# An adapter kept in two tables: biases carried as rows and added by TensorE, two gathers in place of five, the last sequence's base products as tasks of their own

## Chip, cores and metric

The kernel runs on one core of a Trainium2 chip. The metric is the device time of one execution in microseconds (us), the median of several runs. The core has a matrix engine (TensorE, PE in the profile; PEld is its weight load), a vector engine (VectorE, DVE), a scalar engine (ScalarE, ACT), a general engine (GpSimd, POOL) and a queue engine for transfers (SyncE, SP). Matrix products land in PSUM, of which this kernel uses eight banks of 128 x 512 floats.

## What is computed

The reference is one decoder layer on eight sequences of 512 tokens and 256 channels, all in float32: a linear attention with an MLP, a cross-attention over a context of 512 tokens, and a feed-forward part with adapters. Each of the three is followed by x = layernorm(x + part(x)). The change touches the third part only:

```python
base = jnp.einsum('btd,de->bte', x, W_base) + b_base
h = relu(jnp.einsum('btd,ndh->nbth', x, W_enc) + b_enc[:, None, None, :])
recon = jnp.einsum('nbth,nhd->nbtd', h, W_dec) + b_dec[:, None, None, :]
losses = jnp.mean((recon - x[None]) ** 2, axis=(2, 3))
top1 = jnp.argmin(losses, axis=0)
adp = connected_idx[top1]
mid = relu(jnp.einsum('btd,bdr->btr', x, W_down[adp]) + b_down[adp][:, None, :])
adapter_out = jnp.einsum('btr,brd->btd', mid, W_up[adp]) + b_up[adp][:, None, :]
return base + adapter_out
```

For every sequence eight small autoencoders (256 to 64 to 256 channels) try to rebuild the tokens. The one with the smallest error names an adapter, whose two matrices (256 x 64 and 64 x 256) and two biases are then applied to the whole sequence. Which one it is, is known only at run time, so the weights are fetched by an index.

## The kernel before

A sequence x is held as four tiles of 128 tokens x 256 channels (NT = 4). Channels are cut in two chunks of 128 (KC = 2). A float32 product shows as two matrix passes in the profile, so a product over both chunks is four.

**The order of the work** is written by a planner inside the kernel, at build time. Every piece of work is a task (`task`, L112) with an engine, a cost in ns, a due time, what it reads and writes, and the buffers ("rooms") that it fills. `play` (L157) walks through a planned time: whenever an engine is free, it picks, among the tasks that are ready and whose rooms are free, the one with the smallest due time (plus a small bonus or penalty for the change of kind, `SWAY`). It does not look ahead. What it picks is issued at once on that engine, so each engine's order of instructions is the order of the plan, and on the chip each engine follows that order and waits where its data or buffer is late:

```python
fit = [k for k in ready[e]
       if k.at + k.on[e][1] <= now and (port <= now or not alone(k, e)) and roomy(k, now)]
...
k = min(fit, key=lambda k: k.due + SWAY[e].get((was[e], k.kind), 0.0))
```

A task with `others` can go to a second engine after a delay; the bias adds, for instance, are POOL tasks which DVE may take. PSUM has four rooms called "bank" for most products and two double rooms "sc" for attention scores. The queue of SP is planned too: it carries the loads of x and of the context, the stores of the results (L1066, L1060) and the copies of `place` (L904 to L915), 16 transfers which move a transposed block of attention weights into place and which the planner books at 9600 ns.

**The sequences overlap.** Sequence b has its cross-attention in period b (64 x 3.2 us planned); its feed-forward part (`ffn`, L957) runs during the next period, beside the cross-attention of b + 1 and the linear attention of b + 2. Only the last sequence's `ffn` has nothing beside it.

**The steps of `ffn`.** (1) `turn` (L422) transposes x into x2T. (2) Four POOL adds put the base bias on x (L962 to L966; recorded at L377). (3) Four encode products (L973), each for two autoencoders, with a ReLU on ACT (L981) into one of two rooms "he". (4) Eight decode pairs (`decode`, L1070): a pair is two products (L1076) in two banks, which must both be free, each followed by a subtraction on DVE (L1086) into a room "h", of which there are four, and a sum of squares on ACT (L1093). (5) A product with ones (L994) spreads the eight losses over all partitions, and `choose` (L1099) finds the adapter's index with nine small DVE instructions and works out row numbers. (6) Five gathers on POOL (L1001) fetch the down matrix in two halves (128 rows of 64 floats each), the down bias, the up matrix (64 rows of 256 floats) and the up bias, 128 times the same row of 256 floats. (7) The middle product (L1019) with ReLU and bias on ACT (L1023). (8) For each of the four tiles: a POOL add of the up bias to x (L1028, recorded at L377), base and up products in one bank (L1038, L1039), a DVE add to x (L1045) and the statistics of the final norm (L388, L389). (9) The norm: ve on DVE (L397), the power -0.5 on POOL (L402, "rs"), the normalisation (`put`: L410 on DVE, L414 on POOL), and the store. For the last sequence norm and store go tile by tile, for the others all four tiles at once.

The norm that ends the cross-attention has the same form (L397, L402, L410, L414).

Of the kernel before, what the change touches and what calls it, by code (L numbers as in the profile page):

```python
# [9 lines left out]
F32 = mybir.dt.float32  # L10
# [8 lines left out]
P = 128  # L19
# [14 lines left out]
EPS = 1e-5  # L34

# [29 lines left out]
def decoder(ctx: ExitStack, tc: tile.TileContext, t: dict, out: bass.AP):  # L65
# [186 lines left out]
    room("bu", 1, [P, C])  # L252
# [68 lines left out]
    Wbase, bbase = chunked("Wbase", C, C), row("bbase", C)  # L321
# [17 lines left out]
    )  # L339

    row_base = const.tile([P, 4], F32, name="row_base")
    row_step = const.tile([P, 4], F32, name="row_step")
    for j, (start, per, step) in enumerate([(0, 1, C), (P, 1, C), (0, 1, R), (0, 0, 1)]):
        nc.gpsimd.iota(
            row_base[:, j : j + 1],
            [[0, 1]],
            base=start,
            channel_multiplier=per,
            allow_small_or_imprecise_dtypes=True,
        )  # L350
# [606 lines left out]
    def ffn(b, begin, end):  # L957
        x2, x2T, acc, part = xs[b], Val("xT"), Val("acc"), Val("part")
        long = end - begin
        turn(x2T, x2, begin)  # L960
        for c in range(NT):
            task(  # L962
                "pool", 728, begin + (0.1 + 0.05 * c) * long,
                lambda e, c=c: add(e, x2.t[:, c, :], x2.t[:, c, :], bbase),
                [(x2, c)], [(x2, c)], ("bbase",), others=[("dve", 420, 4000)], two=True,
            )  # L966
# [24 lines left out]
        ps_l, bu, mid = Val("bank"), Val("bu"), Val("h")  # L991
# [5 lines left out]
        task("dve", 1900, begin + 0.61 * long, lambda: rows.append(choose(b, ps_l.t)), [(ps_l, 0)], [(chosen, 0)])  # L997
# [9 lines left out]
        every = slice(None)  # L1007
        due = begin + 0.63 * long
        for kc in range(KC):
            task("pool", 1000, due, gather(lambda kc=kc: wd[:, kc, :R], Wdown_rows, every, slice(kc, kc + 1)),  # L1010
                 [(chosen, 0)], [(v_wd, kc)], slack=2000)
        task("pool", 1000, due + 1, gather(lambda: bd[:R], bdown_rows, slice(0, R), slice(2, 3)), [(chosen, 0)], [(v_bd, 0)], slack=2000)
        task("pool", 1000, due + 2, gather(lambda: wu[:R], Wup_rows, slice(0, R), slice(2, 3)), [(chosen, 0)], [(v_wu, 0)], slack=2000)
        task("pool", 1000, due + 3, gather(lambda: bu.t, t["bup"], every, slice(3, 4)), [(chosen, 0)], [(bu, 0)], slack=2000)
        ps_m = Val("bank")

        def middle():
            for kc in range(KC):
                nc.tensor.matmul(ps_m.t, wd[:, kc, :], x2T.t[:, kc, :], start=kc == 0, stop=kc == KC - 1)  # L1019

        task("pe", mm(512, 2), begin + 0.8 * long, middle, chunks(x2T) + each(v_wd, KC), [(ps_m, 0)], kind="full", holds=[mid])
        task(
            "act", 686, begin + 0.82 * long, lambda: nc.scalar.activation(mid.t, ps_m.t, AF.Relu, bias=bd),  # L1023
            [(ps_m, 0), (v_bd, 0)], [(mid, 0)],
        )
        norm = Norm(x2)
        for c in range(NT):
            task(  # L1028
                "pool", 723, begin + 0.8 * long + c,
                lambda e, c=c: add(e, x2.t[:, c, :], x2.t[:, c, :], bu.t),  # L1030
                [(x2, c), (bu, 0)], [(x2, c)], others=[("dve", 420, 4000)], two=True,
            )
            ps = Val("bank")

# [161 lines left out]
```

## Time and profile before

| | us |
|---|---|
| three runs | 1677.8, 1677.01, 1680.26 |
| median | 1677.8 |
| profiled execution, its own time | 1677.12 |
| its span, first to last instruction | 1675.3 |
| busy: PE / DVE / ACT / POOL | 1569.5 / 1320.5 / 1084.0 / 1075.2 |
| mean granted TensorE clock | 0.972 of full speed |

How to read it: an engine line of the page gives busy time and its share of the span. In the view of 40 slices each digit is a busy share in tenths. A group or timeline line has the start, the duration, the engine, the line of the kernel, the operation and the buffers as out<-in, followed by the shape and the number of instructions merged; the bracket holds the time that the engine stood idle before it and what ended that. "SPq" is SyncE's queue of transfers, whose time is that of issuing them. Buffers are named by their rooms, so prods stands for several buffers that share the space of the attention products.

### The profile page before, as it was taken

The page shows a single profiled execution, that of the slowest core. Times are in us where ns is not written, and L with a number is a line of the kernel's source. Part 1 is how long each engine was busy: PE and PEld are TensorE (multiplying, and loading weights), DVE is VectorE, ACT ScalarE, POOL GpSimd, SP SyncE. Part 2 cuts the span into 40 slices and gives each one's busy share as a digit, 9 for nine tenths or more (in the row PEclk, how much of TensorE's full clock was granted, in tenths as well). Part 3 has the DMA queues.
Part 4 walks back from the last instruction along what each step waited for, and adds up shares of the span by engine and source line. Part 5 has one row for each costly group of instructions (what it writes and reads, how often), then busy time and mean ns, then how long its engine had stood idle before and what let it go on. Part 6 is the DMA issues. An engine that isn't in the chain of part 4 may idle for free.

```text
span 1675.3 us, 23902 instructions
## 1 busy us (share of the span) xinstructions
PE 1569.5 (94%) x7856; PEld 935.4 (56%) x7856; DVE 1320.5 (79%) x2261; ACT 1084.0 (65%) x2359; POOL 1075.2 (64%) x881
## 2 busy tenths in 40 slices
PE   4489999999999999999998999989999899999996
PEld 2366666664665555565565565655566554654562
DVE  7987886798889898979976797868969566776554
ACT  1147776678676787678756677657766567646643
POOL 6955886686678697669565794758938241544243
PEclk8689999999999999999999999999999999999998
DMA  8000000022113211221113121221112322333301
GB/s 267 1 1 1 1 1 0 8 54 58 33 34 88 52 26 38 53 75 51 48 29 89 46 52 30 59 79 28 51 35 55 88 72 68 80 100 91 91 7 32
DMA packets 159003, 86.68 MB, mean 52 GB/s; under 512 B 18336, under 2 KB 156192, under 8 KB 158880
## 3 DMA queue, kind: packets, MB, share of 16 engines
q1 hardware_dynamic: 157472, 83.06, 18.4%
q0 software_dynamic: 1408, 2.10, 0.6%
q8 instruction: 63, 1.03, 0.3%
q14 instruction: 60, 0.49, 0.1%
HBM read 16.93 MB, written 4.19 MB: 13 GB/s over the span
## 4 chain that ended last, share of the span: by engine, by line
PE 74%; DVE 10%; SPq 4%; issue 3%; ACT 3%; POOL 3%; DMA 2%; POOLq 0%; DVEq 0%; ACTq 0%
PE sc L847 12%; PE bank L929 12%; PE bank L687 7%; PE bank L662 6%; PE bank L945 5%; PE bank L793 5%; PE bank L893 5%; PE bank L511 4%; SPq L913 4%; PE bank L973 3%; PE bank L800 3%; PE bank L1076 3%; PE bank L809 3%; DVE o L591 2%; ACT p L862 2%
## 5 line engine op out<-in xcount | busy, mean ns | idle before, releaser
L862 ACT ACTIVATE p<-sc,nmax 128x512 f32<-128x512 f32 x512 | 348.1, 689 | 111.3 <-DVE nmax L854 88.6
L873 POOL TENSOR_SCALAR p<-p,rinv 128x512 f32<-128x512 f32 x284 | 204.5, 731 | 325.6 <-DVE rinv L867 316.5
L854 DVE TENSOR_REDUCE nmax<-sc 128x2 f32<-128x1024 f32 x256 | 304.9, 1213 | 82.7 <-PE sc L847 82.0
L559 POOL TENSOR_TENSOR prods<-k,v 128x1088 f32<-128x1088 f32 x119 | 297.5, 2523 | 59.8 <-DVE k L537 32.6
L847 PE MATMUL sc<-kT,qT 64*128 64x512 f32 x1024 | 265.5, 627 | 5.5 <-ACT p L862 4.3
L582 POOL TENSOR_TENSOR prods<-q,kv 128x1088 f32<-128x1088 f32 x95 | 237.4, 2519 | 37.3 <-DVE kv L568 25.6
L568 DVE TENSOR_REDUCE kv<-prods 128x68 f32<-128x1088 f32 x128 | 162.3, 1273 | 10.9 <-POOL prods L559 10.5
L893 PEld LDWEIGHTS bank<-ident,p 128*128 128x128 f32 x1072 | 121.7, 141 | 80.4 <-issue 45.7
L591 DVE TENSOR_REDUCE o<-prods 128x68 f32<-128x1088 f32 x128 | 160.6, 1271 | 4.5 <-POOL prods L582 4.5
L871 ACT ACTIVATE p<-p,rinv 128x512 f32<-128x512 f32 x228 | 155.5, 730 | 3.2 <-DVE rinv L867 2.7
L893 PE MATMUL bank<-ident,p 128*128 128x128 f32 x1072 | 150.3, 277 | 2.6 <-ACT qT L804 1.1
L847 PEld LDWEIGHTS sc<-kT,qT 64*128 64x128 f32 x1024 | 88.7, 190 | 109.6 <-issue 77.2
L929 PE MATMUL bank<-prods,v 128*64 128x256 f32 x1008 | 127.9, 397 | 16.0 <-DMA prods<-blk 14.7
L883 DVE STREAM_TRANSPOSE blk<-p 128x512 f32<-128x512 f32 x184 | 121.9, 689 | 25.7 <-POOL p L873 11.0
L929 PE MATMUL bank<-pT,v 128*64 128x256 f32 x1040 | 128.0, 388 | 4.0 <-DMA prods<-prods 2.1
L793 PE MATMUL bank<-x1T,Wq 128*128 128x512 f32 (+1 forms) x288 | 124.1, 554 | 1.0 <-DVE x L1045 0.5
L945 PE MATMUL bank<-Wo,oT 128*128 128x256 f32 x512 | 121.1, 382 | 0.0
L687 PE MATMUL bank<-projT,h 128*128 128x256 f32 x512 | 119.1, 383 | 1.3 <-ACT h L723 1.3
L687 PEld LDWEIGHTS bank<-projT,h 128*128 128x128 f32 x512 | 95.3, 190 | 26.0 <-issue 9.2
L945 PEld LDWEIGHTS bank<-Wo,oT 128*128 128x128 f32 x512 | 94.8, 190 | 26.5 <-issue 12.1
L929 PEld LDWEIGHTS bank<-prods,v 128*64 128x64 f32 x1008 | 70.2, 141 | 70.6 <-issue 29.6
L372 ACT COPY oT<-bank 128x256 f32<-128x256 f32 x100 | 37.2, 372 | 110.2 <-PE bank L929 109.7
(142 smaller groups left out, 2859.1 us busy)
## 6 DMA issues: line engine op xcount, KB each, us to landing
prods<-blk SPq DMA_DIRECT2D x480, 64.0 KB, 2.1
pT<-blk SPq DMA_DIRECT2D x256, 64.0 KB, 2.1
prods<-prods SPq DMA_DIRECT2D x176, 64.0 KB, 2.1
pT<-prods SPq DMA_DIRECT2D x64, 64.0 KB, 2.1
x<-in_x SPq DMA_DIRECT2D x7, 512.0 KB, 6.5
out<-x SPq DMA_DIRECT2D x7, 512.0 KB, 3.4
ctx<-in_ctxT SPq DMA_DIRECT2D x8, 256.0 KB, 3.1
fcT<-in_fcT SPq DMA_DIRECT2D x1, 1024.0 KB
```

Of the source, the lines that this page charges most:

```text
L559: (nc.gpsimd if e == "pool" else nc.vector).tensor_tensor(pr.t.rearrange("p (d e h) -> p d e h", d=DSPLIT, h=H1), k.t[:, s : s + DSPLIT, : ...
L582: (nc.gpsimd if e == "pool" else nc.vector).tensor_tensor(pr.t.rearrange("p (h e d) -> p h e d", h=DSPLIT, d=D1), q.t[:, s : s + DSPLIT, : ...
L591: nc.vector.tensor_reduce(o.t[:, s : s + DSPLIT, :], pr.t.rearrange("p (h e d) -> p h e d", h=DSPLIT, d=D1), AX.X, ALU.add)
L687: nc.tensor.matmul(ps.t[:, :C], of(f, c), projT[:, f, :], start=f == fs[0], stop=f == fs[-1])
L793: nc.tensor.matmul(ps_q.t[:, :n], Wq[:, kc, cols], x1T.t[:, kc, rows], start=kc == 0, stop=kc == KC - 1)
L847: nc.tensor.matmul(ps.t[:, i, :], qT.t[rows, c * P : (c + 1) * P], kT.t[rows, :], start=True, stop=True)
L854: lambda: nc.vector.tensor_reduce(nmax.t, ps.t, AX.X, ALU.max, negate=True), [(ps, 0)], [(nmax, 0)],
L862: lambda i=i, p=p: nc.scalar.activation(p.t, ps.t[:, i, :], AF.Exp, bias=nmax.t[:, i : i + 1], accum_out=ssum.t[:, i : i + 1]),
L873: nc.gpsimd.tensor_scalar(p.t, p.t, rinv.t[:, i : i + 1], 1.0, ALU.mult, ALU.mult)
L893: nc.tensor.transpose(bank.t[:, m * P : (m + 1) * P], p.t[:, m * P : (m + 1) * P], ident)
L929: nc.tensor.matmul(to, v2.t[:, m, cols], of, start=m == 0, stop=m == NT - 1)
L945: nc.tensor.matmul(ps.t[:, :C], oT.t[:, c * P : (c + 1) * P], Wo[:, pr, :], start=pr == prs[0], stop=pr == prs[-1])
```

## The change

The host lays an adapter out in two tables. `down` has, per adapter, 128 rows of 257 floats: both chunks of the down matrix, padded with zeros from 64 to 128 columns, and as last column the down bias, then ones in rows 64 and 65, then zeros. `up` has 66 rows of 256 floats per adapter: the up matrix, the up bias, the base bias. The ReLU over the middle product, with the last column of `down` as its bias, leaves two rows of ones in mid at 64 and 65, and the up product adds both biases through them. The POOL adds of the base bias and of the up bias go, and so do the load of the base bias and the room "bu". Two gathers fetch what five did. `choose` reads the losses where they lie in PSUM, and its two index steps are folded into one by a second table of -8 to -1, so seven DVE instructions stand for nine; its planned cost goes from 1900 to 1500.

For the last sequence alone (`final`) the tiles go in pairs that share a bank, and the base products become a task without the adapter as input, due at 0.6 of the part's length; the up products are a second task into the same bank. For the other sequences base and up stay one task per tile.

```diff
+UP = 66
...
-    room("bu", 1, [P, C])
...
-    Wbase, bbase = chunked("Wbase", C, C), row("bbase", C)
+    Wbase = chunked("Wbase", C, C)
...
+    iota_low = const.tile([P, NA], F32, name="iota_low")
+    nc.gpsimd.iota(
+        iota_low, [[1, NA]], base=-NA, channel_multiplier=0, allow_small_or_imprecise_dtypes=True
+    )
+    row_base = const.tile([P, 2], F32, name="row_base")
+    row_step = const.tile([P, 2], F32, name="row_step")
+    nc.gpsimd.iota(row_base, [[0, 2]], base=0, channel_multiplier=1, allow_small_or_imprecise_dtypes=True)
+    for j, step in enumerate((P, UP)):
         nc.gpsimd.memset(row_step[:, j : j + 1], float(step))
-    Wdown_rows = t["Wdown"].rearrange("n d r -> (n d) r")
-    Wup_rows = t["Wup"].rearrange("n r d -> (n r) d")
-    bdown_rows = t["bdown"].rearrange("n (r o) -> (n r) o", o=1)
-    wd = const.tile([P, KC, P], F32, name="wd")
+    down_rows = t["down"].rearrange("n p m -> (n p) m")
+    up_rows = t["up"].rearrange("n r d -> (n r) d")
+    wd = const.tile([P, KC * P + 1], F32, name="wd")
     wu = const.tile([P, C], F32, name="wu")
-    bd = const.tile([P, 1], F32, name="bd")
-    for z in (wd, wu, bd):
-        nc.gpsimd.memset(z, 0.0)
+    nc.gpsimd.memset(wu, 0.0)
...
     def ffn(b, begin, end):
         x2, x2T, acc, part = xs[b], Val("xT"), Val("acc"), Val("part")
-        long = end - begin
+        long, final = end - begin, b == B - 1
         turn(x2T, x2, begin)
-        for c in range(NT):
-            task(
-                "pool", 728, begin + (0.1 + 0.05 * c) * long,
-                lambda e, c=c: add(e, x2.t[:, c, :], x2.t[:, c, :], bbase),
-                [(x2, c)], [(x2, c)], ("bbase",), others=[("dve", 420, 4000)], two=True,
-            )
         NG = NA * R // P
         for g in range(NG):
             ps, he = Val("bank"), Val("he")
...
             lambda: nc.vector.tensor_tensor(part.t, acc.t[:, :, 0], acc.t[:, :, 1], ALU.add),
             [(acc, (a, kc)) for a in range(NA) for kc in range(KC)], [(part, 0)],
         )
-        ps_l, bu, mid = Val("bank"), Val("bu"), Val("h")
+        ps_l, mid = Val("bank"), Val("h")
         task(
             "pe", 100, begin + 0.6 * long,
             lambda: nc.tensor.matmul(ps_l.t[:, :NA], ones, part.t, start=True, stop=True), [(part, 0)], [(ps_l, 0)], kind="full",
         )
         rows = []
-        task("dve", 1900, begin + 0.61 * long, lambda: rows.append(choose(b, ps_l.t)), [(ps_l, 0)], [(chosen, 0)])
+        task("dve", 1500, begin + 0.61 * long, lambda: rows.append(choose(b, ps_l.t)), [(ps_l, 0)], [(chosen, 0)])
         def gather(dst, src, lo, hi):
             def emit():
...
             return emit
-        every = slice(None)
         due = begin + 0.63 * long
-        for kc in range(KC):
-            task("pool", 1000, due, gather(lambda kc=kc: wd[:, kc, :R], Wdown_rows, every, slice(kc, kc + 1)),
-                 [(chosen, 0)], [(v_wd, kc)], slack=2000)
-        task("pool", 1000, due + 1, gather(lambda: bd[:R], bdown_rows, slice(0, R), slice(2, 3)), [(chosen, 0)], [(v_bd, 0)], slack=2000)
-        task("pool", 1000, due + 2, gather(lambda: wu[:R], Wup_rows, slice(0, R), slice(2, 3)), [(chosen, 0)], [(v_wu, 0)], slack=2000)
-        task("pool", 1000, due + 3, gather(lambda: bu.t, t["bup"], every, slice(3, 4)), [(chosen, 0)], [(bu, 0)], slack=2000)
+        task("pool", 1000, due, gather(lambda: wd, down_rows, slice(0, P), slice(0, 1)), [(chosen, 0)], [(v_wd, 0)], slack=2000)
+        task("pool", 1000, due + 1, gather(lambda: wu[:UP], up_rows, slice(0, UP), slice(1, 2)), [(chosen, 0)], [(v_wu, 0)], slack=2000)
         ps_m = Val("bank")
         def middle():
             for kc in range(KC):
-                nc.tensor.matmul(ps_m.t, wd[:, kc, :], x2T.t[:, kc, :], start=kc == 0, stop=kc == KC - 1)
-        task("pe", mm(512, 2), begin + 0.8 * long, middle, chunks(x2T) + each(v_wd, KC), [(ps_m, 0)], kind="full", holds=[mid])
-        task(
-            "act", 686, begin + 0.82 * long, lambda: nc.scalar.activation(mid.t, ps_m.t, AF.Relu, bias=bd),
-            [(ps_m, 0), (v_bd, 0)], [(mid, 0)],
+                nc.tensor.matmul(ps_m.t, wd[:, kc * P : (kc + 1) * P], x2T.t[:, kc, :], start=kc == 0, stop=kc == KC - 1)
+        task("pe", mm(512, 2), begin + 0.8 * long, middle, chunks(x2T) + [(v_wd, 0)], [(ps_m, 0)], kind="full", holds=[mid])
+        task(
+            "act", 686, begin + 0.82 * long, lambda: nc.scalar.activation(mid.t, ps_m.t, AF.Relu, bias=wd[:, KC * P :]),
+            [(ps_m, 0), (v_wd, 0)], [(mid, 0)],
         )
         norm = Norm(x2)
-        for c in range(NT):
-            task(
-                "pool", 723, begin + 0.8 * long + c,
-                lambda e, c=c: add(e, x2.t[:, c, :], x2.t[:, c, :], bu.t),
-                [(x2, c), (bu, 0)], [(x2, c)], others=[("dve", 420, 4000)], two=True,
-            )
+        for cs in ((0, 1), (2, 3)) if final else ((0,), (1,), (2,), (3,)):
             ps = Val("bank")
-            def base(c=c, ps=ps):
-                cols = slice(c * P, (c + 1) * P)
-                for kc in range(KC):
-                    nc.tensor.matmul(ps.t[:, :C], x2T.t[:, kc, cols], Wbase[:, kc, :], start=kc == 0, stop=False)
-                nc.tensor.matmul(ps.t[:, :C], mid.t[:, cols], wu, start=False, stop=True)
-            due = begin + (0.86 + 0.03 * c) * long
-            task("pe", mm(256, 3), due, base, chunks(x2T, [c]) + [(mid, 0), (v_wu, 0)], [(ps, 0)], ("Wbase",), "full")
-            task(
-                "dve", 416, due + 0.02 * long,
-                lambda c=c, ps=ps: nc.vector.tensor_tensor(x2.t[:, c, :], x2.t[:, c, :], ps.t[:, :C], ALU.add),
-                [(ps, 0), (x2, c)], [(x2, c)],
-            )
-            norm.stats(c, due + 0.03 * long)
-        final = b == B - 1
+            def base(cs=cs, ps=ps):
+                for n, c in enumerate(cs):
+                    for kc in range(KC):
+                        nc.tensor.matmul(
+                            ps.t[:, n * C : (n + 1) * C], x2T.t[:, kc, c * P : (c + 1) * P], Wbase[:, kc, :],
+                            start=kc == 0 and n == 0, stop=False,
+                        )
+            def up(cs=cs, ps=ps):
+                for n, c in enumerate(cs):
+                    nc.tensor.matmul(
+                        ps.t[:, n * C : (n + 1) * C], mid.t[:, c * P : (c + 1) * P], wu, start=False, stop=c == cs[-1]
+                    )
+            due = begin + (0.86 + 0.03 * cs[-1]) * long
+            if final:
+                task("pe", mm(256, 4), begin + (0.6 + 0.01 * cs[-1]) * long, base, chunks(x2T, cs), [(ps, 0)], ("Wbase",), "full")
+                task("pe", mm(256, 2), due, up, [(mid, 0), (v_wu, 0)], [(ps, 0)], kind="full")
+            else:
+                task("pe", mm(256, 3), due, lambda f=base, g=up: (f(), g()), chunks(x2T, cs) + [(mid, 0), (v_wu, 0)],
+                     [(ps, 0)], ("Wbase",), "full")
+            for n, c in enumerate(cs):
+                task(
+                    "dve", 416, due + 0.02 * long,
+                    lambda n=n, c=c, ps=ps: nc.vector.tensor_tensor(
+                        x2.t[:, c, :], x2.t[:, c, :], ps.t[:, n * C : (n + 1) * C], ALU.add
+                    ),
+                    [(ps, 0), (x2, c)], [(x2, c)],
+                )
+                norm.stats(c, due + 0.03 * long)
...
     def choose(b, ps):
-        loss = small.tile([P, NA], F32, tag="loss", name=f"loss_{b}")
-        nc.vector.tensor_copy(loss, ps[:, :NA])
         least = small.tile([P, 1], F32, tag="least", name=f"least_{b}")
-        nc.vector.tensor_reduce(least, loss, AX.X, ALU.min)
+        nc.vector.tensor_reduce(least, ps[:, :NA], AX.X, ALU.min)
         pick = small.tile([P, NA], F32, tag="pick", name=f"pick_{b}")
-        nc.vector.tensor_scalar(pick, loss, least, -float(NA), ALU.is_equal, ALU.mult)
+        nc.vector.tensor_scalar(pick, ps[:, :NA], least, -float(NA), ALU.is_equal, ALU.mult)
         nc.vector.tensor_tensor(pick, pick, iota_a, ALU.add)
         first = small.tile([P, 1], F32, tag="first", name=f"first_{b}")
         nc.vector.tensor_reduce(first, pick, AX.X, ALU.min)
-        nc.vector.tensor_scalar(first, first, float(NA), None, ALU.add)
-        nc.vector.scalar_tensor_tensor(pick, iota_a, first, cidx, ALU.is_equal, ALU.mult)
+        nc.vector.scalar_tensor_tensor(pick, iota_low, first, cidx, ALU.is_equal, ALU.mult)
         adp = small.tile([P, 1], F32, tag="adp", name=f"adp_{b}")
         nc.vector.tensor_reduce(adp, pick, AX.X, ALU.add)
-        rows = small.tile([P, 4], I32, tag="rows", name=f"rows_{b}")
+        rows = small.tile([P, 2], I32, tag="rows", name=f"rows_{b}")
         nc.vector.scalar_tensor_tensor(rows, row_step, adp, row_base, ALU.mult, ALU.add)
         return rows
...
+    down = np.zeros((NA, P, KC * P + 1), np.float32)
+    for kc in range(KC):
+        down[:, :, kc * P : kc * P + R] = a["ffn_W_down"][:, kc * P : (kc + 1) * P]
+    down[:, :R, -1] = a["ffn_b_down"]
+    down[:, R:UP, -1] = 1.0
+    b_base = np.broadcast_to(a["ffn_b_base"], (NA, 1, C))
+    up = np.concatenate([a["ffn_W_up"], a["ffn_b_up"][:, None], b_base], axis=1)
```

The planner's constants, the periods and everything outside this part are unchanged.

More of the change, by code (lines that the diff above doesn't have):

```diff
@@ L339, in decoder @@
     )
[L341 to L349, printed above, removed]
-        )
+    iota_low = const.tile([P, NA], F32, name="iota_low")
[6 more added lines that the diff above has]
+    for j, step in enumerate((P, UP)):
         nc.gpsimd.memset(row_step[:, j : j + 1], float(step))
-    Wdown_rows = t["Wdown"].rearrange("n d r -> (n d) r")
-    Wup_rows = t["Wup"].rearrange("n r d -> (n r) d")
-    bdown_rows = t["bdown"].rearrange("n (r o) -> (n r) o", o=1)
-    wd = const.tile([P, KC, P], F32, name="wd")
+    down_rows = t["down"].rearrange("n p m -> (n p) m")
+    up_rows = t["up"].rearrange("n r d -> (n r) d")
+    wd = const.tile([P, KC * P + 1], F32, name="wd")
     wu = const.tile([P, C], F32, name="wu")
-    bd = const.tile([P, 1], F32, name="bd")
-    for z in (wd, wu, bd):
-        nc.gpsimd.memset(z, 0.0)
+    nc.gpsimd.memset(wu, 0.0)
     def mm(cols, n):
@@ L1022, in ffn @@
         task(
-            "act", 686, begin + 0.82 * long, lambda: nc.scalar.activation(mid.t, ps_m.t, AF.Relu, bias=bd),
-            [(ps_m, 0), (v_bd, 0)], [(mid, 0)],
+            "act", 686, begin + 0.82 * long, lambda: nc.scalar.activation(mid.t, ps_m.t, AF.Relu, bias=wd[:, KC * P :]),
+            [(ps_m, 0), (v_wd, 0)], [(mid, 0)],
         )
         norm = Norm(x2)
-        for c in range(NT):
-            task(
-                "pool", 723, begin + 0.8 * long + c,
-                lambda e, c=c: add(e, x2.t[:, c, :], x2.t[:, c, :], bu.t),
-                [(x2, c), (bu, 0)], [(x2, c)], others=[("dve", 420, 4000)], two=True,
-            )
-            ps = Val("bank")
-            def base(c=c, ps=ps):
-                cols = slice(c * P, (c + 1) * P)
-                for kc in range(KC):
-                    nc.tensor.matmul(ps.t[:, :C], x2T.t[:, kc, cols], Wbase[:, kc, :], start=kc == 0, stop=False)
-                nc.tensor.matmul(ps.t[:, :C], mid.t[:, cols], wu, start=False, stop=True)
-            due = begin + (0.86 + 0.03 * c) * long
-            task("pe", mm(256, 3), due, base, chunks(x2T, [c]) + [(mid, 0), (v_wu, 0)], [(ps, 0)], ("Wbase",), "full")
-            task(
-                "dve", 416, due + 0.02 * long,
-                lambda c=c, ps=ps: nc.vector.tensor_tensor(x2.t[:, c, :], x2.t[:, c, :], ps.t[:, :C], ALU.add),
-                [(ps, 0), (x2, c)], [(x2, c)],
-            )
-            norm.stats(c, due + 0.03 * long)
@@ L1119, in decoder @@
     xs = [x0] + [Val("x") for _ in range(B - 1)]
-    v_wd, v_bd, v_wu, chosen = Val(None), Val(None), Val(None), Val(None)
+    v_wd, v_wu, chosen = Val(None), Val(None), Val(None)
     PERIOD = 64 * PACE
@@ L1173 @@
         "Wbase": a["ffn_W_base"],
-        "bbase": a["ffn_b_base"],
         "enc": a["ffn_W_enc"].transpose(1, 0, 2).reshape(C, NA * R),
@@ L1178 @@
         "decb": columns(a["ffn_b_dec"]),
-        "Wdown": a["ffn_W_down"],
-        "bdown": a["ffn_b_down"],
-        "Wup": a["ffn_W_up"],
-        "bup": a["ffn_b_up"],
+        "down": down,
+        "up": up,
         "cidx": a["ffn_connected_idx"],
```

## The prediction

> **What bounds the kernel.** I read the page's engine shares and slices first, then busy time in windows of 50 us, then the waits of TensorE and SyncE, then the timelines around the waits found. The first view says who is the bound:
>
> ```profile
> PE 1569.5 (94%) x7856; PEld 935.4 (56%) x7856; DVE 1320.5 (79%) x2261; ACT 1084.0 (65%) x2359; POOL 1075.2 (64%) x881
> PE   4489999999999999999998999989999899999996
> POOL 6955886686678697669565794758938241544243
> ```
>
> TensorE (PE) is busy for 94%, and the change leaves its work alone: 16 base and 8 up passes per sequence stay. So only PE's idle 105.8 us (1675.3 - 1569.5) can move. By the windows, 53.6 us of it lie in the first 100 us and 15.5 after 1650; 36.7 are left for all between. There three windows stand out (columns: stretch; its length; busy of PE, PEld, DVE, ACT, POOL; granted clock; DMA share; GB/s):
>
> ```profile
> 900.00:950.00 50.00, 45.27 (x219) 27.13 (x216) 30.16 (x60) 28.98 (x61) 26.98 (x30) 0.93 0.24 64
> 1100.00:1150.00 50.00, 44.97 (x216) 26.76 (x214) 30.62 (x62) 30.42 (x62) 27.04 (x29) 0.93 0.23 64
> 1300.00:1350.00 50.00, 45.05 (x223) 25.26 (x221) 28.39 (x54) 30.08 (x64) 16.98 (x23) 0.93 0.34 90
> ```
>
> They come a period (198 us) apart. In each, one wait is the cause. Timelines of PE, SyncE's queue and POOL in the first:
>
> ```profile
> 912.11 1.47 PE L893 MATMUL bank<-ident,p 128*128 128x128 f32 x12
> 918.32 3.68 PE L929 MATMUL bank<-prods,v 128*64 128x256 f32 x16 [4.73 <-DMA prods<-blk]
> ```
>
> ```profile
> 905.47 0.39 SPq L1066 DMA_DIRECT2D out<-x  x1
> 906.28 10.27 SPq L913 DMA_DIRECT2D prods<-blk  x16
> ```
>
> ```profile
> 900.52 4.92 POOL L414 TENSOR_SCALAR x<-x,mv,rs 128x256 f32<-128x256 f32 x4
> ```
>
> PE stands still until 16 block copies (L913) have landed. They stood on SP's queue behind the store of the previous sequence (L1066), and that waited for POOL's last normalisation (L414, ends 905.44). The copies' target had been free since the earlier L929 ended at 900.84, and their blocks were ready at 897.8, so the store held them for about 5 us. The three waits are 4.73, 5.03 and 4.95 us. The restart is slow too: L929 took 3.68 us instead of 1.95 and the next scores 3.03 instead of 1.99, 2.8 us more; that is a price of 7.7 us per stall, 23 in all.
>
> The other place is the end, where nothing else covers the last sequence:
>
> ```profile
> 1623.91 0.17 DVE L397 TENSOR_SCALAR ve<-mv 128x4 f32<-128x4 f32 x1
> 1624.34 2.77 POOL L377 TENSOR_TENSOR x<-x,bu 128x256 f32<-128x256 f32 x4 [2.71 <-DMA bu<-in_bup,rows]
> 1627.07 1.04 POOL L402 TENSOR_TENSOR rs<-ve,neghalf 128x4 f32<-128x4 f32 x1
> ...
> 1657.98 3.62 PE L1019 MATMUL bank<-xT,wd 128*128 128x512 f32 x4 [5.07 <-DMA wd<-in_Wdown,rows]
> ...
> 1663.92 2.79 POOL L377 TENSOR_TENSOR x<-x,bu 128x256 f32<-128x256 f32 x4 [2.64 <-DMA bu<-in_bup,rows]
> 1664.69 0.42 DVE L1045 TENSOR_TENSOR x<-x,bank 128x256 f32<-128x256 f32 x1 [9.73 <-POOL x L377]
> ```
>
> Twice the bias adds of L377 are in the way: at 1624 those of sequence 6 hold up the norm of sequence 7, at 1664 those of sequence 7 hold up the first add of the end.
>
> **Edits that cost or save nothing by themselves.** Gone from POOL are 29 base-bias adds (23.9 us; three more ran on DVE, 2.6), 32 up-bias adds (22.3) and 24 gathers (0.90 to 0.95 us and 0.30 of issue each, 29). POOL has 600 us idle, so these 75 us pay only where someone waits for POOL: the two places above. The set-up memsets and iotas end at 2.64 and POOL then waits until 5.57 for DVE, so their loss gains nothing; the base-bias load was first read at 376 us. The first up add no longer follows a POOL add; in the middle of the run that add was done anyway (890.93 against 891.97).
>
> **The chain of an adapter.** Choosing loses the copy (157 ns) and the +8 (154 ns), with their gaps 0.39 us (1652.95 to 1653.15, 1654.01 to 1654.20). The two reductions that now read PSUM I price like the copy that read it: no extra, at most 0.2 us. The middle product waits for one gather instead of two: 1.40 us (881.02 to 882.43). But this gather brings 128 rows of 1028 bytes. No row shows it; the wd rows (256 bytes each) land in 2.5 us, the bu rows (128 times 1024 bytes) in 3.5 to 4.0. I take the bu end, 1.0 later, because of the size; the range keeps 0. Net 0.39 + 1.40 - 1.0 = 0.8 us, up to 1.8. The Trainium skill, "DMA: Bandwidth & Descriptors", How a descriptor splits into AXI transactions, speaks against the change: a row that does not start on a 256-byte boundary costs extra pieces, and 1028-byte rows mostly don't start on one. By it some 0.25 us more would go (estimate from that page: five or six pieces for four), and the net would be 0.55; no row here shows such rows.
>
> **The three stalls.** A store that comes d earlier lets the 16 copies start d earlier, and PE's wait shrinks by d. The planner books a fixed 1000 + 2000 ns per gather and 1900, now 1500, for choosing, so it moves the middle product up by 1.4 us. The x1 projection between it and the base products (L793, 1.88 us) can fall behind them. So d lies between 0 (something else fills in) and 3.3; I take 1.5, near the planner's step. Of the slow restart I take back 0.6 of 2.8, because after a wait of only 2.13 us (PE at 1510.55) L929 still took 3.12: 2.1 us per stall, **-6.3 us** for three; bounds 0 and -23.1. The Trainium skill, "TensorE: Matmul & The Clock Gate", Part 1, says the clock falls after an idle window of about 3.4 us. By it waits of 3.3 us could escape the throttle, and the sum would be -12.9; the row of 1510 speaks against.
>
> **The end, in three terms.**
> First, its start. Without the adds of 1624.34 the inverse root can start right after ve, at 1624.2 instead of 1627.07: 2.9 us. PE has two tiles of sequence 6 (2 x 1.6 us) left that slip in between; part of it is lost. I take **-2.3**, between -1.5 and -2.9.
>
> Second, the base products of the last sequence, now tasks of their own. They move from the end into the decode stage, for the planner takes any task that fits when PE is free. Their due time is last, but a decode pair asks for two banks of four, they ask for one. By the planner's costs, after the third decode pair only one bank is free, and the first base task takes it until the very end; the second does so one pair later. Two banks are left for encode and decode. The stage in numbers (same columns):
>
> ```profile
> 1632.90:1652.30 19.40, 16.75 (x48) 5.59 (x48) 12.14 (x20) 13.84 (x38) 7.16 (x8) 1.00 0.08 28
> ```
>
> PE is idle for 2.65 us here, and four tiles of base products take 4 x 0.86 = 3.4 (1289.26 to 1290.12 for one): at least 0.8 us longer. With two banks a pair also waits for its two evictions (2 x 0.68 us) and an encode in between for its ReLU (0.69): following that order with the durations of the rows, the last square ends 25.3 us after the first encode, not 19.3: 6.0. With the leftover tiles of sequence 6 in between I get 3.5 to 4.6. I take **+4.5**, between 0.8 and 6.0. Nothing covers this; DVE, ACT and then the choosing wait behind it.
>
> Third, the way from the loss to the store. Choosing gives 0.39. The missing second gather gives nothing: the four half-clock products of L1019 (935 to 1192 ns each) ran back to back over it; the wider rows cost 0 to 1.0. The base product ahead of the first up falls out (0.86 to 1.0) and the wait for the bias add too (1663.99 to 1664.69, 0.7). After that DVE sets the pace as before: seven us for four tiles. **-1.4**, between -0.9 and -2.0.
>
> The end together: -2.3 + 4.5 - 1.4 = **+0.8**, between -4.1 and +3.6.
>
> **Sum.** The profiled execution took 1677.1 us (span 1675.3 and 1.8 around it; the median of the runs is 1677.8). 1677.1 - 6.3 + 0.8 = **1671.6 us**.
>
> **Rivals.**
> R1, the stalls vanish: if d reaches 4.9, or the copies are queued before the store, as at 710 to 721 us already. For: the order on SP hangs on one comparison. Against: it needs three times what the chain saves. 1677.1 - 23.1 + 0.8 = 1654.8.
> R2, the shorter chain shortens nothing: the store waits for four POOL normalisations and DVE's statistics, untouched, and the wider gather eats the saving. 1677.1 + 0.8 = 1677.9.
> R3, slower by the banks: the decode stage pays the full 6.0, the start saves 1.5, the end 0.9, and the stalls give nothing: 1677.1 + 3.6 = 1680.7. For: the order read off above. Against: it takes the worst of three ranges at once. It decides if both base tasks stand ahead of the fifth decode pair while the stalls give less than 3.6.
> R4, a fourth stall: from the first changed sequence on every later choice of the planner can flip; at 721 us the store stands just behind the copies. If it goes ahead, 7.7 us: 1677.9 + 7.7 = 1685.6, or 1679.3 with the forecast's gain.
>
> **Chances.** Forecast 0.40 (0.36 of it faster, 0.04 within 0.2%), R1 0.12, R2 0.18 (0.03 faster, 0.12 same, 0.03 slower), R3 0.17 (0.02, rest slower), R4 0.13 (0.01, rest slower). 0.2%, 3.4 us, is about what a measurement of this kernel tells from no change. Faster 0.51, same 0.19, slower 0.30. The range runs from R1 to R4 with some of both left out: 1656 to 1684; the forecast's own is 1665 to 1676.
>
> **What will show it.** Right: PE's waits for the block copies near 918, 1117 and 1314 shrink to 3 to 3.6 us; the last encode stage starts about 2 us sooner; base products lie between the last decodes, which stretch to 22 to 25 us; from the end of the last square (1652.27 before) to the first up add 11 us instead of 12.4. Wrong: waits unchanged, gone, or new ones; base products after the last decode; a gather that lands later than 4 us.

## The result and the profile after

The changed kernel takes 1667.45 us (median of six runs, 1661.63 to 1668.01), the kernel before 1677.4 beside it: a ratio of 0.9932 with a 95% interval of 0.991 to 0.9954, 0.7% faster. The profiled execution took 1667.69 us, span 1665.9 (before 1677.12 and 1675.3). Engine lines of the page after:

```profile
PE 1570.0 (94%) x7856; PEld 934.4 (56%) x7856; DVE 1317.8 (79%) x2229; ACT 1073.2 (64%) x2338; POOL 1030.3 (62%) x826
PE   5489999999999999999999999999999999999995
POOL 6956986686568695769656784768746331443212
```

PE's busy time hardly moved (1569.5 to 1570.0), POOL's fell by 45 us, and three inner slices of PE that were 8s are 9s. The windows of 50 us in which PE had lost about 5 us each, after (same columns as before):

```profile
900.00:950.00 50.00, 49.72 (x257) 31.18 (x255) 40.25 (x88) 30.77 (x62) 30.58 (x32) 1.00 0.23 64
1100.00:1150.00 50.00, 49.77 (x266) 30.01 (x262) 37.78 (x71) 35.25 (x73) 34.98 (x34) 1.00 0.26 72
1300.00:1350.00 50.00, 49.47 (x246) 27.39 (x244) 31.77 (x59) 34.02 (x70) 17.00 (x23) 1.00 0.28 74
```

PE now fills them, at full clock: the stalls are not shorter, as forecast, but gone. SyncE's queue in the first window, after, says why:

```profile
906.80 10.66 SPq L908 DMA_DIRECT2D pT<-blk  x16
917.58 0.52 SPq L1061 DMA_DIRECT2D out<-x  x1
```

The 16 copies go out ahead of the store; before, they stood behind it. The two instruction streams, compared line by line, show this swap at all three places. It was not the planner that made it. The text ahead of the prediction says that SP's queue is planned too. The planner does book it, and in both kernels it puts these copies ahead of the store, but the line `MANUAL` (L17) hands only PE, ACT, DVE and POOL over to the plan. SyncE's order is made by the framework: it had turned the planner's order round at three places before, and did not after. By what comparison it decides was not traced.

Three such swaps should be worth 23 us by the prediction's own price; the kernel gained 9.4 of span. To see where the rest went, I cut the span at ends of output projections of the cross-attention (L945 before, L940 after). From the end of the fourth of these groups to that of the fourteenth lie the same 4823 products of PE in every kernel of this study (one record is missing in some traces); I call it the **middle**. Before, then after (stretch; length; busy of PE, PEld, DVE, ACT, POOL; clock; DMA share; GB/s):

```profile
341.96:1338.84 996.88, 973.96 (x4823) 570.18 (x4823) 835.95 (x1429) 708.07 (x1500) 708.32 (x537) 0.99 0.20 52
```

```profile
341.25:1327.56 986.31, 969.91 (x4823) 565.91 (x4823) 838.93 (x1403) 702.56 (x1488) 684.09 (x512) 1.00 0.20 52
```

The middle gained 10.6 us, all else lost 1.2: 0.7 gained ahead of it, 1.9 lost behind it.

### The profile page after: what moved, and what is told of

Read it like the earlier page. It is cut to its first block, busy times and chain, and to the rows that moved or that the text cites. A ratio compares the mean times of both kernels' runs of the same rounds, so it can differ in the third digit from the quotient of the medians.

```text
span 1665.9 us, 23836 instructions
## 1 busy us (share of the span) xinstructions
PE 1570.0 (94%) x7856; PEld 934.4 (56%) x7856; DVE 1317.8 (79%) x2229; ACT 1073.2 (64%) x2338; POOL 1030.3 (62%) x826
## 4 chain that ended last, share of the span: by engine, by line
PE 68%; DVE 16%; ACT 6%; issue 3%; SPq 3%; DMA 2%; POOL 1%; DVEq 0%; POOLq 0%; ACTq 0%
PE sc L842 11%; PE bank L924 11%; PE bank L682 6%; PE bank L940 5%; PE bank L888 5%; PE bank L657 4%; PE bank L788 4%; PE bank L506 4%; SPq L908 3%; PE bank L962 3%; DVE o L586 3%; PE bank L795 3%; DVE nmax L849 2%; ACT p L857 2%; PE bank L804 2%
## 5 line engine op out<-in xcount | busy, mean ns | idle before, releaser
L868 POOL TENSOR_SCALAR p<-p,rinv 128x512 f32<-128x512 f32 x309 | 218.3, 719 | 314.1 <-DVE rinv L862 289.6
L554 POOL TENSOR_TENSOR prods<-k,v 128x1088 f32<-128x1088 f32 x116 | 290.3, 2524 | 73.9 <-DVE k L532 36.3
L577 POOL TENSOR_TENSOR prods<-q,kv 128x1088 f32<-128x1088 f32 x99 | 250.4, 2547 | 42.9 <-DVE kv L563 25.3
L866 ACT ACTIVATE p<-p,rinv 128x512 f32<-128x512 f32 x203 | 138.9, 728 | 4.0 <-DVE rinv L862 3.8
L924 PE MATMUL bank<-prods,v 128*64 128x256 f32 x1008 | 124.2, 387 | 4.8 <-DMA prods<-blk 2.1
L940 PE MATMUL bank<-Wo,oT 128*128 128x256 f32 x512 | 121.2, 382 | 0.0
L940 PEld LDWEIGHTS bank<-Wo,oT 128*128 128x128 f32 x512 | 94.6, 190 | 28.6 <-issue 14.6
L397 POOL TENSOR_TENSOR rs<-ve,neghalf 128x4 f32<-128x4 f32 (+2 forms) x53 | 50.3, 952 | 94.7 <-DVE ve L392 91.5
L657 PE MATMUL bank<-xT,fcT 128*128 128x512 f32 x224 | 106.3, 601 | 0.7 <-DVE h L1081 0.7
```

Of the source, the lines that this page charges most:

```text
L554: (nc.gpsimd if e == "pool" else nc.vector).tensor_tensor(pr.t.rearrange("p (d e h) -> p d e h", d=DSPLIT, h=H1), k.t[:, s : s + DSPLIT, : ...
L577: (nc.gpsimd if e == "pool" else nc.vector).tensor_tensor(pr.t.rearrange("p (h e d) -> p h e d", h=DSPLIT, d=D1), q.t[:, s : s + DSPLIT, : ...
L868: nc.gpsimd.tensor_scalar(p.t, p.t, rinv.t[:, i : i + 1], 1.0, ALU.mult, ALU.mult)
L924: nc.tensor.matmul(to, v2.t[:, m, cols], of, start=m == 0, stop=m == NT - 1)
L940: nc.tensor.matmul(ps.t[:, :C], oT.t[:, c * P : (c + 1) * P], Wo[:, pr, :], start=pr == prs[0], stop=pr == prs[-1])
```

## Experiments

Twelve kernels, of which the eleventh is the first once more. The kernel before ran at 1677 to 1678 beside most of them, but at 1686 on the chip of kernels 5 to 8; why is not known, so across chips the kernels are compared by the length of the middle. Each length is that of one execution. Kernel 1 and its copy on another chip agree within 0.6 us (975.05 and 974.45), though neither ran on the chip of 5 to 8. For that one there is another pair: kernel 6 ran on it, kernel 9 did not, and they differ only in the three swaps. From the start of the middle to the first of these places they take 569.5 and 569.6 us, between the places 185.4 both, so away from the swaps that chip adds nothing. This table is the summary; PE's idle time is length minus busy:

| kernel | median us | ratio to before, 95% | middle | PE busy in it | idle |
|---|---|---|---|---|---|
| before | 1677.4 | 1 | 996.88 | 973.96 | 22.92 |
| after (the change) | 1667.45 | 0.991-0.9954 | 986.31 | 969.91 | 16.40 |
| before, copies first | 1655.2 | 0.9864-0.990 | 975.05 | 966.24 | 8.81 |
| after, store first | 1689.37 | 1.0062-1.0093 | 1011.47 | 977.11 | 34.36 |
| new parts, old order | 1650.13 | 0.9769-0.9805 | 970.88 | 963.46 | 7.42 |
| the same, store first | 1670.96 | 0.9943-0.9977 | 992.23 | 970.16 | 22.07 |
| old parts, order of 1500 | 1677.25 | 0.9929-0.9961 | 994.47 | 972.86 | 21.61 |
| new parts, order of 1500 | 1659.52 | 0.9871-0.9913 | 982.63 | 969.39 | 13.24 |
| before, copies first, adds out | 1651.1 | 0.9825-0.9861 | 974.00 | 965.44 | 8.56 |

The ratios of kernels 5 to 8 are to the 1686 us of their chip. The trace of "after, store first" is of an execution of 1694.05 us, 4.7 above its median, so its middle is rather too long. The three rows of the middle that the argument on the order rests on, for kernels 1, 6 and 5:

```profile
340.94:1315.99 975.05, 966.24 (x4823) 565.71 (x4823) 835.37 (x1429) 708.59 (x1500) 708.30 (x537) 1.00 0.20 53
341.13:1312.01 970.88, 963.46 (x4822) 566.63 (x4823) 829.15 (x1416) 708.39 (x1500) 664.78 (x485) 1.00 0.20 53
339.71:1334.18 994.47, 972.86 (x4823) 566.13 (x4823) 844.50 (x1428) 703.87 (x1496) 705.00 (x542) 1.00 0.20 52
```

**Theories.** A: the swap on SyncE's queue is the gain, and the rest of the change takes some of it back. Rival B: the shorter chain and the freed POOL are the gain, the swap a by-product.

**1. The kernel before with the copies first.** SyncE is given to the plan; nothing else differs, on any engine, than the three swaps:

```diff
-MANUAL = {ENGINES.PE, ENGINES.Activation, ENGINES.DVE, ENGINES.Pool}
+MANUAL = {ENGINES.PE, ENGINES.Activation, ENGINES.DVE, ENGINES.Pool, ENGINES.SP}
```

> The kernel before with one thing turned round: at three places (the stalls of TensorE at 918, 1117 and 1314 us) SyncE's queue issues the 16 block copies ahead of the previous sequence's store; the order of every instruction on the other engines stays. Theory A (the gain of the change is these three stalls, and the rest of the change costs): the three waits of about 5 us and the slow products behind them are gone, 5 to 7.7 us each, 15 to 23 in all, so 1654 to 1662, below the changed kernel's 1667.5. Theory B (the gain is the shorter chain and the adds and gathers that left POOL; the copies' place is a by-product): at most 4 us come, 1673 to 1677.

1655.2 us, 22 below the kernel before and 12 below the changed kernel. SyncE's queue there:

```profile
900.26 10.52 SPq L913 DMA_DIRECT2D prods<-blk  x16
910.88 0.53 SPq L1066 DMA_DIRECT2D out<-x  x1
```

and the product that had waited 4.73 us:

```profile
912.89 1.95 PE L929 MATMUL bank<-prods,v 128*64 128x256 f32 x16
```

No bracket, and 1.95 us instead of 3.68. The three stretches with a stall shrink by 7.2, 7.2 and 7.6 us: 7.3 each, where the prediction had 7.7. A holds.

**2. The changed kernel with the store first.** Its three groups of copies are held back until the store is issued (and SyncE is in `MANUAL`, so that this stays so):

```diff
+            def store():
+                nc.sync.dma_start(out=out[b].rearrange("(c p) d -> p c d", p=P), in_=x2.t)
+                while HELD:
+                    HELD.pop(0)()
...
+            "sp", 9600, due, (lambda: HELD.append(emit)) if held else emit,
```

> The changed kernel with the three swaps undone: there the 16 copies are issued behind the store again, the order on all other engines stays. Theory A: the three waits of TensorE on the block copies come back, 3.5 to 5 us and the slow products behind each, 12 to 23 us in all, so 1679 to 1690, slower than the kernel before. Theory B: the store now comes earlier relative to its period, so the waits stay under 1 us and the time within 4 us of 1667.5.

1689.37 us, the stalls are back, two of them longer than any in the kernel before (timeline of PE):

```profile
927.25 3.68 PE L928 MATMUL bank<-pT,v 128*64 128x256 f32 x16 [5.88 <-DMA pT<-blk]
...
1127.31 3.45 PE L928 MATMUL bank<-pT,v 128*64 128x256 f32 x16 [4.56 <-DMA pT<-prods]
...
1329.74 3.68 PE L928 MATMUL bank<-pT,v 128*64 128x256 f32 x16 [7.72 <-DMA pT<-blk]
```

Without the swap the change is slower than the kernel before, by 0.8%. B is out. What remains is what takes 12 us back.

**3. and 4. The end.** Kernel 3 undoes the early base products: one task per tile, as in the other sequences (`for cs in ((0,), (1,), (2,), (3,))`, one branch). Kernel 4 keeps the two tasks but lets the base products come after the loss, into the wait for the gather:

```diff
-                task("pe", mm(256, 4), begin + (0.6 + 0.01 * cs[-1]) * long, base, chunks(x2T, cs), [(ps, 0)], ("Wbase",), "full")
+                task("pe", mm(256, 4), begin + (0.6 + 0.01 * cs[-1]) * long, base, chunks(x2T, cs) + [(part, 0)], [(ps, 0)], ("Wbase",), "full")
```

> The changed kernel with the last sequence's base and up products in one task per 128 rows, as in the other sequences: no bank is held through the decode stage. If two held banks are what stretches that stage (theory of the prediction): from the first encode to the end of the last square 19.3 to 21 us instead of 24.0; from there to the end 23 to 25 instead of 22.8, since the base products come back into that way. Sum 1.5 to 4.5 us less, 1663 to 1666. Rival: the stage is long for another reason (the leftover tiles of sequence 6 now lie in it): it stays at 23 to 24, and the total is 1667.5 to 1670.

> The changed kernel with the last sequence's base tasks also reading the sum of squares, so that they come just behind the loss's product, while the gather is on its way. If the held banks stretch the decode stage: it shrinks from 24.0 to 19.5 to 21 us, and TensorE, busy in what was a wait, runs the middle product in 1.9 to 3.0 us instead of 3.75 and the eight up products in less than 3.78. Sum 3 to 6 us less, 1661.5 to 1664.5. Rival: the stage stays long, and only the products at the end get faster, 0.5 to 1.5 us less, 1666 to 1667.

1664.83 us (0.9918 to 0.9953) and 1662.86 us (0.9907 to 0.9941). The end by its marks, worked out from the timelines of PE:

| us | before | after | 3: no early | 4: late |
|---|---|---|---|---|
| last projection to last sequence's first encode | 10.25 | 7.40 | 7.40 | 7.41 |
| first encode to loss product (decode stage) | 19.53 | 24.24 | 20.91 | 20.90 |
| loss product to end of span | 22.78 | 22.54 | 23.79 | 20.75 |

Both shrink the stage by 3.3 us, so the held banks are that much of its 4.7. The other 1.4 is the leftover products of one tile of sequence 6, which in all three lie behind the first encode (after: from 1620.85 to the next product at 1622.24). In the timeline after, the base products stand between the last pairs:

```profile
1631.71 1.13 PE L1071 MATMUL bank<-he,dec 64*128 64x512 f32 x4
1632.77 1.99 PE L1018 MATMUL bank<-Wbase,xT 128*128 128x256 f32 x8
1634.69 1.13 PE L1071 MATMUL bank<-he,dec 64*128 64x512 f32 x4
1635.75 1.99 PE L1018 MATMUL bank<-Wbase,xT 128*128 128x256 f32 x8
```

Moved into the wait, they delay the middle product a little and speed up what follows. The two products after the gather, in the changed kernel:

```profile
1649.18 3.75 PE L1003 MATMUL bank<-xT,wd 128*128 128x512 f32 x4 [5.43 <-DMA wd<-in_down,rows]
1653.76 3.78 PE L1025 MATMUL bank<-wu,h 128*128 128x256 f32 x8 [0.83 <-ACT h L1007]
```

With late base products:

```profile
1639.40 6.53 PE L1018 MATMUL bank<-Wbase,xT 128*128 128x256 f32 x16
1645.77 1.88 PE L1003 MATMUL bank<-xT,wd 128*128 128x512 f32 x4
1648.47 1.99 PE L1025 MATMUL bank<-wu,h 128*128 128x256 f32 x8 [0.83 <-ACT h L1007]
```

The base products run slowly here (granted clock 0.56) and push the middle product back by 1.0 us (6.82 us from the loss product to it, 5.79 in kernel 3). In return it and the up products take half the time, since PE did not stand idle for 5.4 us ahead of them: their granted clock is 1.00, in the changed kernel 0.50. Neither kernel changes the middle (986.01 and 985.94), so the 12 us are not here.

**Theories on the middle.** P: the planner's order, reshuffled by the new costs, costs TensorE many small waits. H: the new instructions themselves cost, the wide gather first.

**5. One planned number.** Kernel 1 with choosing booked at 1500 ns instead of 1900. No piece of work changes, only the order, the buffer that a task gets and, for some tasks, which of its two engines takes it.

```diff
-        task("dve", 1900, begin + 0.61 * long, lambda: rows.append(choose(b, ps_l.t)), [(ps_l, 0)], [(chosen, 0)])
+        task("dve", 1500, begin + 0.61 * long, lambda: rows.append(choose(b, ps_l.t)), [(ps_l, 0)], [(chosen, 0)])
```

> The kernel before with the copies first (median 1655.2), and one number of the plan changed: choosing an adapter is booked with 1500 ns, as in the changed kernel, instead of 1900. Not one instruction is added, removed or altered; only the order in which the planner writes them out can differ. Theory P (what the change gives back in the middle, 11 us between 341 and 1328 us, comes from the reshuffled order alone): the planner's own end moves by 9.7 us, and the chip follows by 5 to 12 us, 1660 to 1667, with many new waits of TensorE of about 1 us and no big one. Theory H (the hardware price of the new parts, such as the wide gather, gives it back): the order hardly matters, 1653 to 1658.

1677.25 us: the middle grew by 19.4 us, above the range of P, twice what the planner itself saw. PE's waits there, the largest sums (line, releaser: us in total, times, longest):

```profile
PE sc L847 <- ACT p L862: 3.0, 4, 1.2
PE bank L929 <- DVE pT L374: 2.7, 1, 2.7
PE bank L628 <- DVE at L603: 2.4, 2, 1.4
PE bank L1038 <- ACT h L1023: 1.8, 2, 1.4
PE bank L893 <- DVE v L527: 1.2, 2, 0.9
```

One is 2.7 us; the rest are different products at different places, each issued a little before its input is there. No single line is a stall; the sum shows it: idle 21.6 us against 8.8, and the same 4823 products busy for 6.6 us more. That second part is no new work. 1.7 us of it are the 16 products behind the wait of 2.7 us, which took 3.63 us instead of 1.95 at a granted clock of 0.54. For the rest, products that start after a wait or in smaller groups have longer records (28 waits instead of 17; four scores take 1.13 us, eight 1.99); this was not added up.

**6. New parts, old order.** The changed kernel's instructions, while the plan still books what it booked before, with tasks that issue nothing in the place of the bias adds and the three gathers (a cut):

```diff
+        for c in range(NT):
+            task("pool", 728, begin + (0.1 + 0.05 * c) * long, nothing, [(x2, c)], [(x2, c)], ("bbase",), others=[("dve", 420, 4000)], two=True)
...
+        task("pool", 1000, due, gather(lambda: wd, down_rows, slice(0, P), slice(0, 1)), [(chosen, 0)], [(v_wd, 0)], slack=2000)
+        task("pool", 1000, due, none, [(chosen, 0)], [(v_wd, 1)], slack=2000)
```

> The changed kernel's instructions in the order that the kernel before has with the copies first: two wide gathers, the short choosing and the products through ones are issued, but the plan still books what the kernel before did (five gathers, eight bias adds per sequence, 1900 ns), and the tasks left over issue nothing. The last base products stay with the up products. Theory P: nothing is given back, 1651 to 1655, at or a little below the 1655.2 of the kernel before with the copies first. Theory H: the new parts carry their price along, and the middle is 5 to 11 us longer, 1660 to 1666.

1650.13 us, just under P's range. The middle is 4.2 us shorter than in kernel 1, not longer. H is out: in the old order the new parts gain.

**7. The same with late base products**, as in kernel 4.

> The same as the changed instructions in the old order, with the last sequence's base products as tasks of their own just behind the loss's product, while the gather is on its way. By the gain seen when only this was moved in the changed kernel (end stretch 49.1 us with it, 52.1 with base and up together): 1 to 3 us less than the old order alone, 1649 to 1653, which would be the fastest of all kernels here. Rival: the order of the end differs and the gain is lost in the scales and puts: the same time as the old order within 1 us.

1646.36 us, the fastest of all (0.974 to 0.9777), 3.8 below kernel 6 where 1 to 3 were expected: 20.3 us from the loss to the end, in place of 23.8.

**8. Other planned costs** for the changed kernel with late base products: choosing 1300, first gather 600, second 2000 ns, and SyncE in `MANUAL`.

> The changed kernel with the late base products, the planned order on SyncE's queue too, and three planned costs changed (choosing 1300 ns, first gather 600, second 2000): all instructions are those of the changed kernel, the planner's own end is 1641.9 us, below that of the kernel before (1643.2) and 3.2 below the 1645.2 of the late-base kernel (median 1662.9). Theory P: the chip follows the plan at least in sign, 1652 to 1660. Theory H: the price stays, within 2 us of 1662.9. If neither holds and it is slower than 1665, the planner's own end is no guide to the chip's time within some us.

1660.48 us, half a us above P's range and 2.4 under the kernel that H refers to, with nothing gained in the middle (985.32): it decides nothing between them. But the plan with the earliest own end (1641.9) is 14 us behind kernel 7 on the chip, whose own end is 1643.4. So the order costs, but the planner's own end does not tell by how much.

**9. The case that the prediction priced:** kernel 6 with the store first (held back as in kernel 2).

> The changed kernel's instructions in the old order, with the three groups of copies held back behind the store, as the kernel before has them. This is the case that the prediction priced: same order, same place of the copies, only a shorter chain from the loss to the store. If the prediction's step holds (each wait shrinks by d, 1.5 us, 2.1 with the restart), TensorE's three waits measure 3 to 3.7 us instead of 4.7 to 5.0, and the middle (from the end of the projection at 341 us to that at 1339, 996.9 us in the kernel before) takes 988 to 993. Rival: the store comes 3 to 4 us earlier, as the gap from the loss to the last normalised tile did in the changed kernel (27.3 to 23.8 us): the waits fall below 2 us and the middle to 976 to 984.

1670.96 us, middle 992.23. The waits of PE:

```profile
916.42 3.68 PE L930 MATMUL bank<-prods,v 128*64 128x256 f32 x16 [4.82 <-DMA prods<-blk]
...
1113.92 3.68 PE L930 MATMUL bank<-prods,v 128*64 128x256 f32 x16 [5.23 <-DMA prods<-blk]
...
1310.94 3.41 PE L930 MATMUL bank<-prods,v 128*64 128x256 f32 x16 [4.51 <-DMA prods<-blk]
```

The length lies in the first expectation's range, but the waits fit neither: 14.6 us in all, against 14.7 before. At the first two places the store does come sooner after the loss (26.5 us instead of 27.3), but PE arrives sooner by nearly as much (34.7 instead of 35.4). At the third PE arrives as before (34.7), the store 0.3 sooner, and the wait is 0.4 shorter. So the 4.7 us by which the middle is shorter were gained outside these waits.

**10. New parts in the order of 1500.** Kernel 6 with that one number.

> The changed instructions in the old order (middle of 970.9 us, median 1650.1), with choosing booked at 1500 ns in the plan instead of 1900 and nothing else: the fourth case beside the old parts in the order of 1900 (middle 975.1) and of 1500 (994.5), and the new parts in that of 1900. Theory P, the order alone costs, whatever the parts: the middle takes 986 to 991, 15 to 20 us more than with 1900. Rival: with the shorter chain of the new parts the shorter booking is the true one, and the order of 1500 suits them: 971 to 978.

Middle 982.63, 11.8 us more than with 1900: between the two expectations. That order costs both sets of parts, the old ones more (19.4) than the new.

**11. Kernel 1 again, on another chip.**

> The kernel before with the copies ahead of the stores once more, on the chip of these runs, because the kernel before itself differed by 9 us between two chips (1677.2 and 1686.0). Expected: below the kernel before by 20 to 25 us where that runs at 1677, by 28 to 33 where it runs at 1686 (the stalls, and not the rest, being what is longer there); the middle again 975 us, within 0.5.

1656.12 us beside 1678.08 of the kernel before (0.9849 to 0.9889): 22.0 us again, and the middle 974.45, a hair outside the half us expected. This was not the chip on which the kernel before took 1686, so what is longer there stays open.

**12. Only the bias adds out.** In kernel 1, the two `add` calls of `ffn` become `lambda e: None`, so its output lacks both biases.

> The kernel before with the copies first, and the 64 bias adds of the base layer and the adapter left out (they stay in the plan and issue nothing, so the order of all else is the same; the two biases are missing from the output). The five gathers and the long choosing stay. In the old order the new parts saved 4.2 us of the middle (975.05 to 970.88, 4823 products in both). Prediction on record: adds on POOL cost nothing there. If that is right, the middle stays at 974 to 975.5 and the 4.2 us belong to the gathers and the choosing. Rival: the adds hold up the sums that free the banks, and the base products wait for those: 970.5 to 972, so the adds carry nearly all of it. At the end, without the adds in front of the last norm, the first encode starts 2 us sooner in both cases.

Middle 974.00, 0.5 to 1.1 us less than kernel 1: so some 3 of the 4.2 us belong to the three missing gathers and the shorter choosing (which of the two was not separated), and the adds are nearly free, as predicted. At the end the last encode starts 2.0 us sooner (8.24 us after the last projection instead of 10.26), as expected.

## Why the prediction was right in its number, and where it was wrong

1667.45 lies in the range, 4.2 us below the forecast, but it got there another way. The middle as a ledger, from the lengths above: copies first **-21.8** (996.88 to 975.05), new parts **-4.2** (to 970.88), new order **+15.4** (to 986.31). Sum -10.6; the prediction had -6.3. That the number came out so near is luck: two terms that the sum did not have, -21.8 and +15.4, nearly cancelled.

- **What bounds the kernel**: TensorE, with the same work, is right. That only its idle 105.8 us can move is not: in the middle the idle time fell by 6.5 us (22.92 to 16.40), and the busy time of the same products by 4.1 (973.96 to 969.91).
- **The price of a stall**, 7.7 us with its slow restart: 7.3 measured, and 7.1 in kernel 9 against kernel 6.
- **"A store that comes d earlier lets the 16 copies start d earlier, and PE's wait shrinks by d"**: this step failed. In kernel 9 d is 0.8, 0.8 and 0.3 us (the net 0.8 of the chain, not the 1.5 taken near the planner's step), and the waits together are unchanged, since at two of the three places PE arrives earlier too. The middle's gain there (4.7, with -6.3 forecast) comes from elsewhere, so the size is near for a wrong reason. In the changed kernel the step does not apply, for the copies are ahead.
- **Rival R1, the copies queued before the store**: this is what happened. I held its chance at 0.12, on the ground that it needs three times what the chain saves. That counts for a planner that compares times; the queue's order was not the planner's, and I had read `MANUAL` too fast.
- **"From the first changed sequence on every later choice of the planner can flip"** (R4): right, but I priced it as one more stall. It came as 9.0 us more idle time, in waits of up to 1.3 us for twenty-odd different inputs, and 6.4 us more busy time of the same products, at a granted clock of 1.00 in both (kernel 6 to the changed kernel): 15.4, the largest loss of the change, and the term that was missing from the sum. Kernel 5 shows that one booked number is enough for such a loss; which of the three that changed here (choosing, gathers, missing adds) does most was not separated.
- **Edits at nothing**: bias adds 0.5 to 1.1 us, right within what can be told. For the gathers and the choosing I gave nothing in the middle beyond d; with the small rest of the adds they are 3 us.
- **R2**, nothing gained at the stalls, is out. **R3**, slower by the banks, had the mechanism but not the whole price.
- **Start of the last encode** -2.3: measured -2.85. **Banks held in the decode stage** +4.5: measured +4.7, with the base products exactly between the last pairs; kernels 3 and 4 show that 3.3 of it is the banks.
- **From the loss to the store** -1.4: measured -0.24. Two costs were missed: the gather starts 0.81 us after the row numbers instead of 0.30 (why was not found; at the other adapters it is 0.30, but for 0.84 at the second, where POOL was still busy), and the first up product to the first add takes 2.11 us instead of 1.29, because two tiles now share a task and run at a granted clock of 0.50. The wide gather itself is cheaper than I took it: from issue to landing 3.2 us in the median, 0.6 over the narrow one (2.6), not 1.0.
- The Trainium skill, "DMA: Bandwidth & Descriptors", How a descriptor splits into AXI transactions, was weighed against these rows. The unaligned rows of 1028 bytes landed in 3.2 us, those of 1024 bytes (the up bias, one row 128 times) in 3.8: no run here shows the extra pieces as time.

## What to carry to other kernels

Find out who orders each queue, not only who books it: three groups of 16 copies, each behind a store, were worth 22 us, and the edit that gets them is one word. When a change alters what a planner books, price it in the old order first, with tasks that issue nothing, and then look for the order: here the parts gain 4 us, the new order costs 15. Work that waits for nothing belongs into a wait, not in front of work that shares its buffers.

## What was not expected of the hardware

A wait of about 2 us slows TensorE in some executions and not in others. The same product, after nearly the same wait, in kernel 1 (granted clock 1.00) and in its copy on another chip (0.58):

```profile
1487.64 1.95 PE L929 MATMUL bank<-pT,v 128*64 128x256 f32 x16 [2.05 <-DMA prods<-prods]
```

```profile
1488.55 3.33 PE L929 MATMUL bank<-pT,v 128*64 128x256 f32 x16 [2.20 <-DMA prods<-prods]
```

It is not the length that decides: at this place kernel 7 shows 3.52 us after a wait of 1.62, kernel 10 shows 1.95 after 1.61. The Trainium skill, "TensorE: Matmul & The Clock Gate", Part 1, has the clock watched in a window of about 3.4 us that runs freely, which would make the outcome a matter of where in the window the wait falls. The page asks for a whole idle window, though; here 2.2 us, or 1.6, were enough at times, with a wait of 0.92 us and 1.13 us of products just ahead. So the prediction was right to go by the row and not by the rule, but the row is not a fixed price: it is paid in some executions.
